# Batch 0's keys by block products, with the sums they need moved ahead of them

## The chip, the core and the metric

The kernel runs on one core of one Trainium2 chip, in 32-bit floats throughout. The metric is the device time of one execution in microseconds (us), given as the median of several runs. In the profile PE is TensorE's matrix multiplier and PEld its weight loads, DVE is VectorE, ACT is ScalarE, POOL is GpSimd, SP is SyncE; a trailing q (SPq, ACTq) is the engine's own instruction queue, where it issues DMAs. L465 is line 465 of the kernel's text.

## The reference

A cross attention with two branches over 16 batches of 100 query rows of width 640, with 8 heads of width 80. Cut to what matters:

```python
enc, ca = encoder_hidden_states[:, :718], encoder_hidden_states[:, 718:]
keyt, valt = enc @ Wk, enc @ Wv                      # (16, 718, 640) each
hs = mha(x @ Wq, keyt, valt)
ca_q1 = einsum('btc,th->bch', ca, Wq_ca)[:, indices]  # 100 of 384 rows
ca_hs1 = mha(ca_q1, x, x)
ca_hs2 = mha(ca_hs1 @ Wq, ca @ Wk_ca, ca @ Wv_ca)
out = (hs + ca_hs2) @ Wout + b_out + x
```

The part that is changed computes keyt for batch 0: the encoder's 718 rows of width 384, times Wk of 384 by 640, kept transposed as the tile kT.

## The kernel before

**Stages.** A prologue (about the first 60 us) loads the weights, makes the values of batch 0 partly (L375), folds the second branch's weights (L1242, L1265), turns Wk (L1288), and makes the keys and queries of batch 0 (L666, L535). Then a loop over the 16 batches: scores (L716), maxima and exponentials, the second branch's softmaxes, and, in between, the keys and values of the following work, so that TensorE has a product to run while the other engines make the softmax. Instructions of the prologue are put into order by a scheduler, which keeps dependences and may move independent instructions; `issue_after(x)` holds a group back until x has been issued on its engine. The loop is issued in the order of the text.

**Keys by 15 block products.** For all batches but the first, the class Keys (L453) makes four of the five 128-row chunks of kT. It takes the encoder rows as three parts u and three width chunks c, and the weights as three chunks c and two halves g, a 3x3 by 3x2 block product. This needs 18 block products written out, and 15 by a scheme of the fast matrix product kind: 15 forms of the inputs (A_AT, enc_sums, L481) times 15 forms of the weights (W_AT, weight_sums, L502), whose products are added up in banks A to E of PSUM and moved to kT by a copy on ScalarE (L407) the first time and by an add on VectorE (L405) after that. K_PLAN lists the order: bank, form, and the part of kT that the bank is added to after it. One block product is two matmul instructions of 240 columns. 13 Pool instructions of 128x240 make a batch's input forms; 12 VectorE instructions of 128x256 make the weights' forms, once. The fifth chunk is made plainly by last_keys (L691): nine instructions with the weights wk4.

**Batch 0's keys before.** first_keys (L684) makes all five chunks plainly through chunk_keys (L661), 5 x 9 matmul instructions of 240 columns, and ten copies on ScalarE (L677). weight_sums was split: the forms that overwrite no raw weights (late=False) run before first_keys' products in the text, the five that do (late=True: 5, 7, 13, 3, 14) after them.

**Second branch of batch 0.** keys(load_m(b)) (L848) writes five masked pieces into the tile m2 on Pool, one for each chunk c. Second.products (L874) multiplies x by them into y_ps, ten instructions; VectorE copies the first T = 4 columns of each head into g (L890), ScalarE the rest into y (L896). scores1 (L898) makes e1 on Pool from g in seven instructions (four products L905, three adds L912), and softmax1 (L916) takes it over on VectorE. m2 is one tile for all batches, so batch 1's masks can only follow batch 0's products.

**Copies of wq.** 15 VectorE copies (L1299, L1305) rearrange wq as its five pieces land, ahead of the weight sums.

**PSUM.** psum() hands out banks of two pools of two in turn (psumk, psum1), which y_ps, w_ps (the turned weights), the kT_ps and k_ps banks, va_ps and q_ps share.

Of the kernel before, what the change touches and what calls it, by code (L numbers as in the profile page):

```python
# [8 lines left out]
F32 = mybir.dt.float32  # L9
AF = mybir.ActivationFunctionType  # L10
ALU = mybir.AluOpType
# [3 lines left out]
B, S, H = 16, 100, 640  # L15
NH, D = 8, 80
CAD, T = 384, 4
SK = 722 - T
P = 128
HC = H // P  # L20
CC = CAD // P
# [32 lines left out]
for h in range(NH):  # L54
    lo = h * D
    while lo < (h + 1) * D:
        c = lo // P
        hi = min((h + 1) * D, (c + 1) * P)
        PIECES.append((h, c, lo - h * D, lo - c * P, hi - lo))
        lo = hi  # L60
# [3 lines left out]
HG = T + HT  # L64
# [58 lines left out]
NF = len(V_PLAN)  # L123
# [3 lines left out]
def kernel(  # L127
# [18 lines left out]
    nc = tc.nc  # L146
# [5 lines left out]
    small = ctx.enter_context(tc.tile_pool(name="small", bufs=1))  # L152
# [18 lines left out]
    def psum1(name):  # L171
        return ps1.tile([P, 512], F32, tag="ps1", name=name)
# [3 lines left out]
    def psum(name):  # L176

        turn[0] += 1
        return (psumk if turn[0] % 2 else psum1)(name)
# [28 lines left out]
    def enc_tile(name):  # L208

        return inp.tile([P, NF, KT], F32, tag="enc", name=name)  # L210

    def rest_tile(name):
        return main.tile([P, len(A_REST), KT], F32, tag="rest", name=name)
# [23 lines left out]
    def a_raw(enc, u, c):  # L237
        if (u, c) in A_REST:
            return enc[1][:, A_REST[u, c]]
        return enc[0][:, A_RAW[u, c]]  # L240

    def a_form(enc, f):
        return enc[0][:, A_AT[f]]
# [8 lines left out]
    wk_sb = const.tile([P, NF, 2, P], F32, name="wk_sb")  # L252
# [11 lines left out]
    enc = enc_tile("enc_0"), rest_tile("rest_0")  # L264
# [216 lines left out]
    def enc_sums(enc):  # L481

        at = lambda f: a_form(enc, f)
        raw = lambda u, c: a_raw(enc, u - 1, c - 1)
        for out, left, right, op in (
            (at(7), raw(2, 3), raw(3, 1), ALU.add),
            (at(11), raw(3, 2), raw(3, 3), ALU.add),
            (at(8), at(11), raw(2, 3), ALU.subtract),
            (at(10), raw(1, 3), at(11), ALU.subtract),
            (at(9), raw(2, 1), raw(2, 2), ALU.add),  # L490
            (at(2), raw(1, 1), at(9), ALU.subtract),
            (at(9), at(9), raw(3, 1), ALU.subtract),
            (at(5), raw(1, 1), raw(2, 1), ALU.subtract),
            (at(5), at(5), raw(2, 3), ALU.add),
            (at(11), raw(1, 3), raw(3, 3), ALU.subtract),
            (at(11), at(11), raw(3, 1), ALU.add),
            (at(4), at(2), at(10), ALU.add),
            (at(4), at(4), raw(1, 2), ALU.add),
        ):
            nc.gpsimd.tensor_tensor(out, left, right, op)  # L500

    def weight_sums(engine, w, late=None, there={}):  # L502


        at = lambda f: there.get(f, w[:, W_AT[f]])
        raw = lambda c, g: w[:, 2 * (c - 1) + g - 1]
        for f, left, right in (
            (0, raw(1, 2), raw(1, 1)),
            (11, raw(2, 2), raw(3, 2)),
            (12, raw(3, 2), raw(3, 1)),  # L510
            (5, raw(2, 2), raw(1, 2)),
            (7, raw(3, 2), at(5)),
            (13, raw(3, 1), at(7)),
            (1, raw(2, 1), raw(3, 1)),
            (3, raw(1, 1), at(7)),
            (6, raw(2, 1), raw(1, 1)),
            (10, raw(3, 1), raw(2, 2)),
            (2, raw(1, 1), raw(2, 2)),
            (14, raw(2, 1), raw(2, 2)),
        ):  # L520
            if late is None or late == (f in (5, 7, 13, 3, 14)):
                engine.tensor_tensor(at(f), left, right, ALU.subtract)


    def queries_tiles(p):
# [135 lines left out]
    def chunk_keys(n, banks, weights, enc):  # L661
        copies = []
        for bank, thirds in zip(banks, ((0, 1), (2,))):
            for i, u in enumerate(thirds):
                for c in range(CC):
                    nc.tensor.matmul(  # L666
                        bank[:, i * KT : (i + 1) * KT],
                        weights[c],
                        a_raw(enc, u, c),
                        start=(i == 0 and c == 0),  # L670
                        stop=(c == CC - 1),
                        skip_group_check=True,
                    )
        for bank, thirds in zip(banks, ((0, 1), (2,))):
            w = len(thirds)
            copies.append(
                nc.scalar.copy(  # L677
                    kT[:, n, thirds[0] : thirds[0] + w],
                    bank[:, : w * KT].rearrange("p (u k) -> p u k", u=w),
                )  # L680
            )
        return copies

    def first_keys(enc):  # L684
        for n in range(HC - 1):
            banks = [psum(f"kT_ps_0_{n}_{k}") for k in range(2)]
            weights = [wk_sb[:, 2 * c + n % 2, n // 2] for c in range(CC)]
            chunk_keys(n, banks, weights, enc)
        last_keys(0, enc)

    def last_keys(b, enc):  # L691
        banks = pair(f"kT_ps_{b}")
        return chunk_keys(
            HC - 1,
            [banks[:, k] for k in range(2)],
            [wk4[:, c] for c in range(CC)],
            enc,
        )
# [140 lines left out]
    def load_m(b):  # L839
        if b < 2:  # L840
            return lambda c: m_sb[c][:, b * HT : (b + 1) * HT]
        mb = small.tile([P, HC, HT], F32, tag="mb", name=f"mb_{b}", bufs=2)
        nc.sync.dma_start(
            out=mb, in_=m_d[:, :, b * HT : (b + 1) * HT].rearrange("c p n -> p c n")
        )
        return lambda c: mb[:, c]

    def keys(m):  # L848

        for c, heads in enumerate(HEADS):  # L850
            n = len(heads)
            nc.gpsimd.tensor_tensor(
                m2[:, c, :n, T:],
                m(c).unsqueeze(1).to_broadcast([P, n, HT]),
                hmask[:, c, :n].unsqueeze(2).to_broadcast([P, n, HT]),
                ALU.mult,
            )

    class Second:

# [13 lines left out]
        def products(self):  # L874

            b = self.b
            y_ps = psum1(f"y_ps_{b}")
            for c, heads in enumerate(HEADS):
                for lo, hi in QC:
                    nc.tensor.matmul(  # L880
                        y_ps[lo:hi, heads[0] * HG : (heads[-1] + 1) * HG],
                        self.xT[:, c, lo:hi],
                        m2[:, c, : len(heads)].rearrange("p h k -> p (h k)"),
                        start=(c == 0),
                        stop=(c == HC - 1),
                        skip_group_check=True,
                    )
            self.g = g = small.tile([S, NH, T], F32, tag="g", name=f"g_{b}")
            y_v = y_ps[:S, : NH * HG].rearrange("p (h k) -> p h k", h=NH)
            summed = nc.vector.tensor_copy(g, y_v[:, :, :T])  # L890
            self.y_v = y_v
            return summed

        def copy(self):
            self.y = y_sbs[self.b % 2]
# [353 lines left out]
    k2T, at = [], 0  # L1249
# [26 lines left out]
        )  # L1276
        nc.sync.dma_start(out=m_d[c], in_=m_sb[c])
    second = Second(0, xT, ca_0)
    keys(load_m(0))
    summed = second.products()  # L1280
    second.copy()
    second.scores1()
    keys(load_m(1))

    for c in range(HC):
        w_ps = psum(f"w_ps_{c}")
        for cc in range(CC):
            nc.tensor.transpose(  # L1288
                w_ps[:, cc * P : (cc + 1) * P], wkt_sb[:, c, cc * P : (cc + 1) * P], ident
            )  # L1290
        act(
            wk_sb[:, c % 2 : 6 : 2, c // 2] if c < HC - 1 else wk4,
            w_ps[:, : CC * P].rearrange("p (a n) -> p a n", a=CC),
        )

    with tc.issue_after(summed.ins):
        for c in range(HC):
            for r in range(2):
                nc.vector.tensor_copy(  # L1299
                    wq_sb[:, c, : 4 * P].rearrange("p (n r k) -> p n r k", n=RG, r=2)[  # L1300
                        :, :, r
                    ],
                    wq_in[c].rearrange("p (r n k) -> p r n k", r=2, n=RG)[:, r, :, :64],
                )
            nc.vector.tensor_copy(  # L1305
                wq_sb[:, c, 4 * P :].rearrange("p (h k) -> p h k", h=NH),
                wq_in[c].rearrange("p (h k) -> p h k", h=NH)[:, :, 64:],
            )
    with tc.issue_after(summed.ins):
        weight_sums(nc.vector, wk_sb, False)  # L1310
    first_keys(enc)
    weight_sums(nc.vector, wk_sb, True)

    va = wide("va")[:, : H // 2]
    va_ps = psum("va_ps")
# [34 lines left out]
    for b in range(B):  # L1350
        p = b // 2
        e_in, now = enc, second
        enc, second = enc_next, second_next
# [220 lines left out]
        for g in range(2):  # L1574
# [3 lines left out]
            order = [(h, i) for h in range(4 * g, 4 * g + 4) for i in range(len(KC))]  # L1578
# [95 lines left out]
```

## Time and profile before

| | |
|---|---|
| three runs | 919.67, 921.84, 922.21 us; median 921.84 |
| the profiled execution | 919.14 us |
| its span, first to last instruction | 917.4 us |
| TensorE's granted clock in it | 0.999 |
| busy in 0 to 30 us | PE 27.14, DVE 10.55, ACT 5.17, POOL 15.22 us |
| busy in 30 to 52 us | PE 22.00, DVE 12.15, ACT 6.84, POOL 17.27 us |

The span is the time from the first to the last instruction on the core; the device time is 1.7 us longer. Rows of a timeline give the start, the duration, the engine, the line, the operation, the tiles written and read, their shape and how many instructions are merged in the row; in brackets stands how long the engine was idle before it and what ended that. Every 32-bit matmul instruction appears as two passes, so that x90 is 45 instructions.

### The profile page before, as it was taken

Reading aid. Unit: us, or ns where it says so; the run is one execution under the profiler, and the core shown is the slowest. Engines: PE = TensorE matmul, PEld = TensorE weight load, DVE = VectorE, ACT = ScalarE, POOL = GpSimd, SP = SyncE. Lnnn points to the kernel's source line nnn. Section 1 sums busy time; section 2 is a strip of 40 time slices with the busy share of each in tenths; the row PEclk is TensorE's granted clock in tenths of the full one; section 3 lists DMA queues with packets and bytes.
Section 4 is the critical chain, followed back from the end, with each engine's and each line's share of the span. In section 5 each row is a group of like instructions: output and inputs, shape, how many; then the busy total and the mean of one; then the engine's idle time right before and its main releaser. Section 6 shows DMA issues by size and latency. Waiting matters only on the chain.

```text
span 917.4 us, 27706 instructions
## 1 busy us (share of the span) xinstructions
PE 910.1 (99%) x11974; PEld 765.7 (83%) x11974; DVE 692.3 (75%) x1116; ACT 434.3 (47%) x836; POOL 706.2 (77%) x659
## 2 busy tenths in 40 slices
PE   9999999999999999999999999999999999999998
PEld 6988889797797979888798787988879788797966
DVE  3459795989759897795967869679785898748883
ACT  2234533737337363652737436264741737426341
POOL 5749999687968879696896969958797687966623
PEclk9999999999999999999999999999999999999999
DMA  9822112031201302230121301203130032210211
GB/s 269 272 77 78 48 32 67 26 104 53 85 28 45 85 29 78 54 100 35 47 60 54 104 32 52 55 24 106 53 81 31 24 106 53 82 46 24 61 45 39
DMA packets 50581, 62.94 MB, mean 69 GB/s; under 512 B 13682, under 2 KB 37810, under 8 KB 50460
## 3 DMA queue, kind: packets, MB, share of 16 engines
q1 hardware_dynamic: 48812, 59.18, 21.6%
q8 instruction: 94, 1.54, 0.7%
q10 hardware_dynamic: 1024, 1.15, 0.4%
q0 software_dynamic: 624, 0.85, 0.3%
q14 instruction: 27, 0.22, 0.1%
HBM read 55.59 MB, written 5.57 MB: 67 GB/s over the span
## 4 chain that ended last, share of the span: by engine, by line
PE 99%; DMA 0%; issue 0%; DVE 0%; POOL 0%; ACTq 0%; POOLq 0%
PE s_ps L716 12%; PE a_ps L1586 12%; PE v_psA L434 11%; PE v_psB L434 9%; PE k_psA L465 8%; PE kT_ps L666 8%; PE k_psB L465 7%; PE o_ps L1164 5%; PE v_psC L434 4%; PE k_psC L465 3%; PE v_ps L375 2%; PE q_ps L593 2%; PE q_ps L535 2%; PE v_psD L434 2%; PE v_psE L434 2%; PE q_psA L593 1%
## 5 line engine op out<-in xcount | busy, mean ns | idle before, releaser
L905 POOL TENSOR_TENSOR e<-ca,g 100x800 f32<-100x800 f32 x64 | 97.9, 1541 | 100.0 <-ACT kT L407 54.6
L500 POOL TENSOR_TENSOR enc<-enc 128x240 f32<-128x240 f32 x135 | 109.0, 817 | 18.3 <-DMA enc<-in_enct 11.1
L1372 DVE TENSOR_TENSOR st<-st,over 120x1600 f32<-120x1600 f32 x48 | 113.3, 2362 | 0.0
L1586 PEld LDWEIGHTS a_ps<-vs,st 120*36 120x36 f32 (+3 forms) x3072 | 109.3, 124 | 3.5 <-issue 3.4
L1586 PE MATMUL a_ps<-vs,st 120*36 120x81 f32 (+3 forms) x3072 | 111.7, 233 | 0.0
L434 PE MATMUL v_psA<-wv_sb,enc 128*120 128x320 f32 x352 | 109.3, 433 | 0.0
L1011 POOL TENSOR_TENSOR hs<-hs,hs 100x640 f32<-100x640 f32 x48 | 94.8, 1974 | 3.8
L912 POOL TENSOR_TENSOR e<-e,e 100x800 f32<-100x800 f32 x48 | 93.6, 1950 | 3.8
L1004 POOL TENSOR_TENSOR hs<-vb,p 100x640 f32<-100x640 f32 x64 | 91.1, 1433 | 3.9 <-DMA vb<-va_d 1.0
L434 PE MATMUL v_psB<-wv_sb,enc 128*120 128x320 f32 x296 | 91.8, 433 | 0.0
L465 PE MATMUL k_psA<-enc,wk_sb 128*128 128x240 f32 x360 | 89.3, 370 | 0.0
L1380 ACT ACTIVATE st<-st 120x1600 f32<-120x1600 f32 x48 | 73.9, 1539 | 29.6 <-DVE st L1372 29.0
L434 PEld LDWEIGHTS v_psA<-wv_sb,enc 128*120 128x120 f32 x352 | 64.2, 183 | 25.0 <-DVE vs L405 0.5
L465 PEld LDWEIGHTS k_psA<-enc,wk_sb 128*128 128x128 f32 x360 | 67.2, 190 | 15.2 <-issue 0.2
L1384 DVE TENSOR_TENSOR most<-most,st 120x800 f32<-120x800 f32 x64 | 65.0, 1015 | 15.4 <-ACT st L766 14.2
L716 PE MATMUL s_ps<-qp,kT 64*56 64x100 f32 (+1 forms) x3072 | 73.1, 248 | 0.0
L465 PE MATMUL k_psB<-enc,wk_sb 128*128 128x240 f32 x300 | 73.0, 366 | 0.0
L434 PEld LDWEIGHTS v_psB<-wv_sb,enc 128*120 128x120 f32 x296 | 54.1, 183 | 21.9 <-DVE vs L405 0.4
L716 PEld LDWEIGHTS s_ps<-qp,kT 64*56 64x56 f32 (+1 forms) x3072 | 66.9, 130 | 5.4 <-issue 4.2
L1079 ACT COPY hsT<-turned_hs 32x160 f32<-32x160 f32 (+7 forms) x244 | 67.7, 278 | 3.0
L772 ACT COPY st<-s_ps 120x800 f32<-120x800 f32 x64 | 49.8, 830 | 34.3 <-PE s_ps L716 34.3
L465 PEld LDWEIGHTS k_psB<-enc,wk_sb 128*128 128x128 f32 x300 | 57.0, 190 | 7.7
(200 smaller groups left out, 1847.0 us busy)
## 6 DMA issues: line engine op xcount, KB each, us to landing
vb<-va_d SPq DMA_DIRECT2D x62, 250.0 KB
enc<-in_enct SPq DMA_DIRECT2D x30, 240.0 KB
enc<-in_enct SPq DMA_DIRECT2D x15, 360.0 KB
xT<-in_xt SPq DMA_DIRECT2D x8, 500.0 KB
rest<-in_enct SPq DMA_DIRECT2D x31, 120.0 KB
xn<-in_x SPq DMA_DIRECT2D x11, 320.0 KB
out<-xn SPq DMA_DIRECT2D x11, 320.0 KB
ca<-in_cas SPq DMA_DIRECT2D x16, 156.2 KB
```

What stands on the lines that cost most here:

```text
L434: nc.tensor.matmul(at[0][j][:KN, : H // 2], a_form(self.enc, f)[:, j * KN : (j + 1) * KN], wv_there.get(f, wv_sb[:, W_AT[f]]), start=first ...
L465: nc.tensor.matmul(at[:, i * KT : (i + 1) * KT], wk_sb[:, W_AT[f], i], a_form(self.enc, f), start=(first and i == 0), stop=last, skip_grou ...
L500: nc.gpsimd.tensor_tensor(out, left, right, op)
L666: nc.tensor.matmul(bank[:, i * KT : (i + 1) * KT], weights[c], a_raw(enc, u, c), start=(i == 0 and c == 0), stop=(c == CC - 1), skip_group ...
L716: nc.tensor.matmul(s_ps[at][k0:k1, cols], w, rhs, start=not begun & {(at, k) for k in range(k0, k1, 32)}, stop=last, skip_group_check=True,)
L905: first = nc.gpsimd.tensor_tensor(to, self.ca[:, t, :].unsqueeze(1).to_broadcast([S, NH, S]), g[:, :, t].unsqueeze(2).to_broadcast([S, NH, ...
L912: nc.gpsimd.tensor_tensor(e, e, to, ALU.add)
L1004: first = nc.gpsimd.tensor_tensor(to, self.vb[t][:S].rearrange("p (h d) -> p h d", h=NH), p2[:, :, t].unsqueeze(2).to_broadcast([S, NH, D] ...
L1011: nc.gpsimd.tensor_tensor(sums, sums, to, ALU.add)
L1372: return nc.vector.tensor_tensor(st[i], st[i], top.over[:KN].unsqueeze(1).to_broadcast([KN, 2, ROWS]), ALU.subtract,)
L1380: nc.scalar.activation(st[i], st[i], AF.Exp, scale=SCALE)
L1586: nc.tensor.matmul(a_v[lo:hi, h % 4], st[i // 2][: KEYS[i], i % 2, h * S + lo : h * S + hi], block(i, h // 4)[: KEYS[i], h % 4], start=(i ...
```

## The change

It makes batch 0's first four chunks of keys by Keys, as for the other batches, and no longer by first_keys. What goes with it:

- enc_sums(enc) for batch 0: 13 more instructions on Pool, in its order ahead of batch 0's masks.
- Batch 0's masks come first, then batch 1's, which are now held until batch 0's last mask has been issued. Before, the scheduler had four of batch 1's ahead of batch 0's last one.
- g is copied in two parts for batch 0: heads 0 to 6 right after the products, head 7 behind all twelve weight sums, and scores1 on Pool reads both.
- All twelve weight sums stand behind the last copy of wq, in one row, ahead of batch 0's products.
- The turned weights are made in the order 4, 0, 1, 2, 3, so that wk4 is there first, and last_keys(0) runs ahead of the block products.
- On SyncE the load of x for batches 2 and 3 (xT) comes ahead of that of batch 1's ca.

From batch 0's scores on, all engines have the same instructions in the same order as before.

```diff
@@ weight_sums
-                engine.tensor_tensor(at(f), left, right, ALU.subtract)
+                made = engine.tensor_tensor(at(f), left, right, ALU.subtract)
+        return made
@@
-    def first_keys(enc):
-        for n in range(HC - 1):
-            banks = [psum(f"kT_ps_0_{n}_{k}") for k in range(2)]
-            weights = [wk_sb[:, 2 * c + n % 2, n // 2] for c in range(CC)]
-            chunk_keys(n, banks, weights, enc)
-        last_keys(0, enc)
-
@@ keys
-            nc.gpsimd.tensor_tensor(
+            made = nc.gpsimd.tensor_tensor(
...
+        return made
@@ Second.products
-            self.g = g = small.tile([S, NH, T], F32, tag="g", name=f"g_{b}")
-            y_v = y_ps[:S, : NH * HG].rearrange("p (h k) -> p h k", h=NH)
-            summed = nc.vector.tensor_copy(g, y_v[:, :, :T])
-            self.y_v = y_v
-            return summed
+            self.g = small.tile([S, NH, T], F32, tag="g", name=f"g_{b}")
+            self.y_v = y_ps[:S, : NH * HG].rearrange("p (h k) -> p h k", h=NH)
+            if b > 0:
+                self.take(0, NH)
+
+        def take(self, lo, hi):
+            return nc.vector.tensor_copy(self.g[:, lo:hi], self.y_v[:, lo:hi, :T])
@@ prologue
-    keys(load_m(0))
-    summed = second.products()
+    enc_sums(enc)
+    masked = keys(load_m(0))
+    second.products()
+    summed = second.take(0, NH - 1)
     second.copy()
-    second.scores1()
-    keys(load_m(1))
-
-    for c in range(HC):
+
+    order = (HC - 1, *range(HC - 1))
+    for c in order:
         w_ps = psum(f"w_ps_{c}")
...
-            nc.vector.tensor_copy(
+            moved = nc.vector.tensor_copy(
                 wq_sb[:, c, 4 * P :].rearrange("p (h k) -> p h k", h=NH),
...
-    with tc.issue_after(summed.ins):
-        weight_sums(nc.vector, wk_sb, False)
-    first_keys(enc)
-    weight_sums(nc.vector, wk_sb, True)
+    with tc.issue_after(moved.ins):
+        made = weight_sums(nc.vector, wk_sb)
+    with tc.issue_after(made.ins):
+        second.take(NH - 1, NH)
+    second.scores1()
+    with tc.issue_after(masked.ins):
+        keys(load_m(1))
+    last_keys(0, enc)
+    Keys(0, enc).go(NF)
```

## The prediction

> **What bounds the kernel now.** First the page: span, engines, the chain that ended last.
>
> ```profile
> span 917.4 us, 27706 instructions
> PE 910.1 (99%) x11974; PEld 765.7 (83%) x11974; DVE 692.3 (75%) x1116; ACT 434.3 (47%) x836; POOL 706.2 (77%) x659
> PE 99%; DMA 0%; issue 0%; DVE 0%; POOL 0%; ACTq 0%; POOLq 0%
> ```
>
> TensorE (PE) is busy 910.1 of 917.4 us and the chain that ended last is 99% PE. A busy PE need not be a PE at its peak, so the second view is who PE waited for, over the whole run.
>
> ```profile
> PE idle_ps L1230 <- DVE idle L1227: 1.1, 1, 1.1
> PE y_ps L880 <- POOL m L852: 0.7, 1, 0.7
> PE z_ps L934 <- issue: 0.6, 2, 0.3
> PE v_ps L375 <- DMA wv_sb<-in_wv: 0.6, 1, 0.6
> PE m_ps L1265 <- issue: 0.5, 1, 0.5
> ```
>
> Its waits come to 3.5 us. Work taken off PE therefore shortens the run one for one, unless a new wait takes its place, and one of these five waits (y_ps on Pool, 0.66 us) lies in the stage that is changed. Third, the chain in order of time through that stage and into batch 0.
>
> ```profile
> 28.61 0.86 POOL m L852 x3
> 29.86 1.46 PE w_ps L1288 x12
> 31.32 18.23 PE kT_ps L666 x90
> 49.55 1.77 PE va_ps L1318 x12
> 82.35 0.81 PE k_psB L465 x4
> ```
>
> Each matmul instruction is recorded as two passes. Batch 0's keys are 45 instructions, 90 passes, 18.23 us: 0.2026 us a pass. The same block products that the change brings to batch 0 already run for batch 1 (k_psB): four passes, 0.81 us, the same price per pass.
>
> **The change part by part.** *Fewer products.* first_keys made 4 chunks of 9 instructions. Keys makes 15 products of 2. That is 6 instructions, 12 passes, 12 x 0.2026 = 2.43 us off PE. The last chunk's 9 instructions stay, and now run first.
>
> *Masks by batch.* Rows of the timeline (start, duration, engine, line):
>
> ```profile
> 27.66 0.69 DVE L1273 COPY m<-m_ps 128x512 f32<-128x512 f32 x1 [0.63 <-PE m_ps L1265]
> 28.31 0.55 PE L1288 MATMUL w_ps<-ident,kT 128*128 128x128 f32 x3
> 28.31 1.16 POOL L852 TENSOR_TENSOR m<-m,hmask 128x96 f32<-128x96 f32 x4
> 29.52 0.34 PE L880 MATMUL y_ps<-m,xT 128*64 128x72 f32 x4 [0.66 <-POOL m L852]
> 30.02 5.28 POOL L852 TENSOR_TENSOR m<-m,hmask 128x64 f32<-128x64 f32 x1 [0.56 <-PE y_ps L880]
> ```
>
> m's last chunk is copied by 28.35, but Pool had batch 1's masks ahead of batch 0's last one, so the last y_ps product waited to 29.52. With batch 0's five first, that mask runs 28.4 to 28.7, before PE has ended its transposes at 28.86: 0.66 us off PE. Everything after it moves up by 0.66: the other 12 transposes end at 31.32 - 0.66 = 30.66, the last chunk's 18 passes (3.65 us) at 34.31.
>
> *Weight sums, now all before the products.* Product one needs form 7, the sixth of the twelve sums. The sums stand on VectorE (DVE) behind the copies of wq.
>
> ```profile
> SPq L1277 <- DMA wq<-in_wq: 0.4, 1, 0.4
> 31.96 0.33 SPq L1277 DMA_DIRECT2D m_d<-m  x1
> 32.17 0.49 DVE L1299 COPY wq_sb<-wq 128x256 f32<-128x256 f32 x2
> 32.71 2.44 DVE L522 TENSOR_TENSOR wk_sb<-wk_sb 128x256 f32<-128x256 f32 x7
> L522 DVE TENSOR_TENSOR wk_sb<-wk_sb x12: 420/425/1912, 32.7 to 48.3; 128x256 f32<-128x256 f32 x12
> ```
>
> The copies too would start 0.66 earlier, but SyncE's store at 31.96 waits 0.4 for the fifth piece of wq to land (the row above it), so its copies start at 31.98 at best, and the sums 0.54 behind (32.71 - 32.17): 32.52. One sum takes 0.425, seven take 2.44, so 0.336 from start to start. The sixth ends at 32.52 + 5 x 0.336 + 0.425 = 34.62; with some 0.1 for the signal PE waits from 34.31 to 34.7. Cost 0.4 us, and between 0 (the piece landed earlier than the store shows) and 1.35 (0.95 of Pool's masks in between, below). I take 0.4, because the store's row is the only one that dates the piece. Forms 13 and 3, the eighth and ninth sums, end at 35.3 and 35.6, and PE needs them at 35.5 and 37.1.
>
> *The products close together.* From 34.7 PE has 30 x 0.405 = 12.15 us of products, to 46.9. Each bank is read by ScalarE or DVE before it is used again:
>
> ```profile
> 83.20 0.56 ACT L407 COPY kT<-k_psB 128x480 f32<-128x480 f32 x1 [0.25 <-PE k_psB L465]
> 84.83 0.66 DVE L405 TENSOR_TENSOR kT<-k_psA,kT 128x480 f32<-128x480 f32 x1
> ```
>
> Nine adds of 0.66 and six copies of 0.56 stand beside 12.15 us of PE. Walking the plan A B D A B E A B A C B C A B C A product by product (E and C are split in two), the tightest is bank B's fourth use: DVE adds A, E, B in a row, 3 x 0.66 us, and ends some 0.3 us before PE comes. I cost it at 0; with each add 0.1 slower PE would lose under 0.1.
>
> *Sums of batch 0's encoder rows: 13 new Pool instructions, ahead of its masks.* Nearest are the same sums for batch 1.
>
> ```profile
> 13.37 0.16 POOL L365 MEMSET y_sb<- 100x8 f32 x2
> 17.24 1.11 SPq L301 DMA_DIRECT2D kT<-in_wkt  x2
> 19.03 0.59 SPq L301 DMA_DIRECT2D kT<-in_wkt  x1
> 23.15 0.29 POOL L852 TENSOR_TENSOR m<-hs_sb,hmask 128x64 f32<-128x64 f32 x1 [9.63 <-DVE hs_sb L1273]
> 58.83 0.69 POOL L500 TENSOR_TENSOR enc<-enc 128x240 f32<-128x240 f32 x1 [11.15 <-DMA enc<-in_enct]
> 106.30 2.80 POOL L500 TENSOR_TENSOR enc<-enc 128x240 f32<-128x240 f32 x2
> ```
>
> Pool is idle from 13.5 to 23.15. Four sums read only what had landed for the values: 13.5 to 16.3 at 0.70. The fifth and sixth need the first third of the rows; the SyncE issues at 17.75, 18.4 and 19.03 each wait for one piece of it, and show no wait, so it is there by then. Nine more at 0.7 end at 23.7 to 25.3. The fourth mask can't start before 27.1 anyway and the third not before 25.8, so there is room of 1 to 2 us, and the cost is 0. DVE's copies there read PSUM; beside DVE work on SBUF a sum takes 1.40 (2.80 for two), and that is a rival.
>
> *g in two parts.* g's last column block comes behind the twelve sums, so Pool's scores1 starts later.
>
> ```profile
> 35.26 3.03 POOL L905 TENSOR_TENSOR e<-ca,g 100x800 f32<-100x800 f32 x2
> 45.69 0.32 SPq L870 DMA_DIRECT2D ca<-in_cas  x1
> 45.74 1.94 POOL L912 TENSOR_TENSOR e<-e,e 100x800 f32<-100x800 f32 x1
> 45.13 3.63 DVE L522 TENSOR_TENSOR wk_sb<-wk_sb 128x256 f32<-128x256 f32 x4 [2.81 <-PE kT_ps L666]
> 48.67 1.01 DVE L807 STREAM_TRANSPOSE turned<-e 128x800 f32<-128x800 f32 x1
> 51.35 1.82 SPq L219 DMA_DIRECT2D enc<-in_enct  x3
> 52.82 0.98 DVE L834 COPY spread<-mx 128x800 f32<-128x800 f32 x1
> 56.34 1.01 DVE L837 STREAM_TRANSPOSE over<-spread 128x800 f32<-128x800 f32 x1 [2.53 <-DMA va_d<-va]
> 63.85 0.88 ACT L927 ACTIVATE e<-e 100x800 f32<-100x800 f32 x1
> ```
>
> The sums end at 32.52 + 11 x 0.336 + 0.425 = 36.6; then g, and what is left of batch 1's masks on Pool (0.6): scores1 runs 37.3 to 49.7 (12.4 us as before), 2.0 later than before. Behind it, one queue at a time. DVE: transpose to spread take 5.1 us (48.67 to 53.8 before), so the next transpose starts at 54.9 and e1 is ready at 56.9; ScalarE reads it at 63.85 - 2.7 = 61.2. SyncE: ca's load waits for scores1's last product, to 47.7, and batch 1's rows behind it for the va products, to 48.7; xT now goes ahead of ca. So the rows still go 2.7 us earlier, and Pool's sums for batch 1 start at 58.83 - 2.7 = 56.1, long after 49.7. Cost 0, with 4 us of cover on the e1 side and 1.0 on ca's; beyond these the delay reaches batch 1's rows first. In exchange no sum sits beside scores1, as the four at 45.13 did, of which one took 1.9 us.
>
> *Sum:* 2.43 + 0.66 - 0.4 = 2.7 us. The profiled execution took 919.14 us (917.4 and 1.7 around the span), so 916.4 by its own measure. It is lower than all three runs (919.67, 921.84, 922.21); the mean of the four executions is 920.7, and from that I forecast **918.0**.
>
> **The rivals.** (1) *The wait for form 7 doesn't come*: wq's fifth piece lands before 31.6. For it: SyncE dates a landing from above only. Gain 3.1: 917.6.
>
> (2) *Pool's masks of batch 1 take turns with DVE.* Three of them (0.29 to 0.35 us) are still queued when DVE begins its copies at 29.4. If each goes between two DVE instructions, form 7 is 0.95 later and the gain is 1.7: 919.0. Against it: the mask at 30.02 needed 5.28 us, because it stood aside until DVE's stream ended at 35.15, and no instruction of that stream got longer. [...]
>
> (3) *Slower: the sums of batch 0 hold Pool past its masks.* If they run at the 1.40 us of the row at 106.30 and the first third lands only at 19.0, nine sums end at 31.6, the five masks (0.32 each) at 33.2, and the last y_ps product goes at 33.25 instead of 29.52: 3.73 lost against 2.43, slower by 1.3: 922.0. It decides once the sums end after 30.3. Against it: DVE works from PSUM there, and the sums beside such work took 0.7.
>
> (4) *The gain is eaten downstream*: e1 or batch 1's rows come late because scores1 starts 2.0 later, and PE waits in batch 0. It needs another 4 us on the e1 side. Time 920.7, no change.
>
> **How the numbers follow.** Forecast 0.66, (1) 0.12, (2) 0.10, (3) 0.07, (4) 0.05. A measurement of this kernel can tell about 0.3% (2.8 us) from no change; the runs shown spread 2.5 us. Against the median 921.84 the bound is 919.1: forecast and (1) end below it about 7 times in 10, (2) about half the time: faster 0.60. (3) and an unknown like it make slower 0.08, and 0.32 stays the same. The range goes from 919.14 - 3.1 = 916.0, less 0.4 of scatter, 915.6, to 922.21 less the 0.9 that the least lucky of the faster cases would leave, 921.3.
>
> **What would show it.** Right: 78 passes between the transposes and va; va's products start near 46.9; y_ps waits for no mask; Pool's batch 0 sums end before 25.8; PE waits 0.3 to 0.5 us for L522 ahead of the first k_psA; scores1 starts near 37; no new PE wait later. Wrong: PE idle ahead of y_ps with Pool still in L500 (3); a wait of over 1 us for L522, with masks between DVE's instructions (2); PE idle ahead of z_ps or batch 1's k_ps (4); kT adds over 0.8 us and PE waiting between the products.

## The result and the profile after

| | before | after |
|---|---|---|
| median of nine runs | 920.94 us (917.72 to 923.77) | 916.66 us (916.04 to 919.66) |
| ratio after to before | | 0.9958, 95% interval 0.9942 to 0.9975 |
| the profiled execution | 919.14 us | 916.04 us |
| its span | 917.4 us | 914.1 us |

Faster by 0.42%, 1.3 us below the forecast of 918.0 and inside its range. Two more sets, run with the experiments on other chips, gave less: 0.9981 (0.9972 to 0.9991) and 0.9980 (0.9970 to 0.9989), 1.7 to 1.8 us by these ratios and 1.4 us between the medians. Both the stage that was meant and a loss behind it can be read in the profile.

First, PE's busy line of the page and PE's waits over the whole run, changed kernel.

```profile
PE 908.2 (99%) x11962; PEld 762.8 (83%) x11962; DVE 699.0 (76%) x1126; ACT 434.2 (47%) x834; POOL 706.8 (77%) x672
```

```profile
PE k_psB L465 <- DVE sm L983: 0.3, 1, 0.3
```

The twelve passes are gone (11974 to 11962), and so is the y_ps wait on Pool. A new one is there that nobody ordered: k_psB, behind a VectorE instruction of batch 0's softmax. Next, rows of the timeline from 13 to 50 us (start, duration, engine, line, operation; in brackets the idle time ahead of it and what ended it).

```profile
17.97 2.00 POOL L500 TENSOR_TENSOR enc<-enc 128x240 f32<-128x240 f32 x3 [1.85 <-DMA enc<-in_enct]
...
23.96 0.29 POOL L846 TENSOR_TENSOR m<-hs_sb,hmask 128x64 f32<-128x64 f32 x1
...
28.48 0.29 POOL L846 TENSOR_TENSOR m<-m,hmask 128x64 f32<-128x64 f32 x1 [0.97 <-PE y_ps L875]
28.84 0.34 PE L875 MATMUL y_ps<-m,xT 128*64 128x72 f32 x4
...
32.44 4.10 DVE L522 TENSOR_TENSOR wk_sb<-wk_sb 128x256 f32<-128x256 f32 x12
33.89 0.57 PE L667 MATMUL kT_ps<-rest,wk 128*128 128x240 f32 x2
34.58 1.08 PE L465 MATMUL k_psA<-enc,wk_sb 128*128 128x240 f32 x4
...
36.69 3.04 POOL L902 TENSOR_TENSOR e<-ca,g 100x800 f32<-100x800 f32 x2 [6.28 <-DVE g L889]
```

Pool's sums end where the first mask starts, at 23.96. The last y product goes at 28.84 (29.52 before). The last chunk's last two passes start at 33.89; two passes take 0.41, so the next could start at 34.3, but k_psA comes at 34.58: 0.3 us of waiting for form 7 (its cause is read off below). From there the products run without a gap, and va follows at 46.93 on the timeline; in the chain of waits it stands at 47.00, before at 49.55: 2.55 us gained.

What made the wait for form 7 can be read from Pool's and VectorE's rows of the same execution, and from SyncE's:

```profile
29.16 1.25 POOL L846 TENSOR_TENSOR m<-m,hmask 128x96 f32<-128x96 f32 x4
...
29.34 0.62 DVE L1297 COPY wq_sb<-wq 128x256 f32<-128x256 f32 x2
...
30.17 0.60 DVE L1297 COPY wq_sb<-wq 128x256 f32<-128x256 f32 x2
...
31.90 0.48 DVE L1297 COPY wq_sb<-wq 128x256 f32<-128x256 f32 x2
...
31.22 0.33 SPq L1274 DMA_DIRECT2D m_d<-m  x1
```

VectorE's fifteen copies of wq run without a gap, so here it waits for no piece of wq; SyncE's store, by which the prediction dated the fifth piece, goes at 31.22, ahead of that piece's copies at 31.90. But the first copies run beside Pool's masks of batch 1: a pair takes 0.62 and 0.60 us, and 0.48 once the masks are over at 30.41. From the first copy to the first sum it is 3.10 us (29.34 to 32.44), against 2.69 in the kernel before (30.02 to 32.71). The masks cost VectorE 0.41 us. Without them the sixth sum would by these rows end at 34.1, before PE is ready at 34.3 (an estimate).

That gain stands until batch 0's loop and shrinks there. The chain in order of time, changed kernel, start and length of each piece:

```profile
63.79 1.51 DVE most L1387
65.32 1.37 DVE most L1387
67.37 0.91 DVE most L1387
68.30 2.22 DVE most L1387
...
80.43 1.05 PE k_psB L465 x4
```

From 60 to 80 us the chain is no longer PE's: it runs through VectorE, above all through its maxima (L1387). In the kernel before, the maxima, Pool's first two products of scores1 and k_psB of the same place stood as follows:

```profile
69.39 2.38 DVE L1384 TENSOR_TENSOR most<-most,st 120x800 f32<-120x800 f32 x2
...
72.03 3.05 POOL L905 TENSOR_TENSOR e<-ca,g 100x800 f32<-100x800 f32 x2
...
82.19 0.97 PE L465 MATMUL k_psB<-enc,wk_sb 128*128 128x240 f32 x4
```

There Pool's products start behind the maxima. Its k_psB started at 82.19, so at 80.43 only 1.76 of the 2.55 us are left.

### The profile page after: what moved, and what is told of

Its sections match the earlier page's. It is cut to its first block, busy times and chain, and to the rows that moved or that the text cites. A ratio compares the mean times of both kernels' runs of the same rounds, so it can differ in the third digit from the quotient of the medians.

```text
span 914.1 us, 27711 instructions
## 1 busy us (share of the span) xinstructions
PE 908.2 (99%) x11962; PEld 762.8 (83%) x11962; DVE 699.0 (76%) x1126; ACT 434.2 (47%) x834; POOL 706.8 (77%) x672
## 3 DMA queue, kind: packets, MB, share of 16 engines
q10 hardware_dynamic: 1024, 1.15, 0.4%
## 4 chain that ended last, share of the span: by engine, by line
PE 96%; DVE 3%; ACT 0%; issue 0%; DVEq 0%
PE a_ps L1589 12%; PE s_ps L710 12%; PE v_psA L434 11%; PE v_psB L434 9%; PE k_psA L465 8%; PE k_psB L465 7%; PE kT_ps L667 6%; PE o_ps L1161 5%; PE v_psC L434 4%; PE k_psC L465 3%; PE q_ps L594 2%; PE q_ps L536 2%; PE v_psE L434 2%; PE v_psD L434 2%; PE v_ps L375 2%; PE q_psA L594 1%
## 5 line engine op out<-in xcount | busy, mean ns | idle before, releaser
L500 POOL TENSOR_TENSOR enc<-enc 128x240 f32<-128x240 f32 x144 | 113.3, 797 | 14.7 <-DMA enc<-in_enct 7.5
L465 PE MATMUL k_psA<-enc,wk_sb 128*128 128x240 f32 x384 | 95.3, 371 | 0.1
L465 PEld LDWEIGHTS k_psA<-enc,wk_sb 128*128 128x128 f32 x384 | 71.5, 190 | 16.3 <-DVE wk_sb L522 0.5
L1387 DVE TENSOR_TENSOR most<-most,st 120x800 f32<-120x800 f32 x64 | 66.3, 1036 | 15.9 <-ACT st L760 14.7
L465 PE MATMUL k_psB<-enc,wk_sb 128*128 128x240 f32 x320 | 78.0, 366 | 0.3 <-DVE sm L983 0.3
L465 PEld LDWEIGHTS k_psB<-enc,wk_sb 128*128 128x128 f32 x320 | 60.7, 190 | 8.6 <-issue 0.7
```

Of the source, the lines that this page charges most:

```text
L465: nc.tensor.matmul(at[:, i * KT : (i + 1) * KT], wk_sb[:, W_AT[f], i], a_form(self.enc, f), start=(first and i == 0), stop=last, skip_grou ...
```

## The experiments

Line numbers of the runs are their own; the operation and the tile say which is which. All runs with a ratio were timed against the kernel before on the same chip.

**hold.** Batch 0 calls scores1 for batch 1 as the later batches do.

```diff
         if b == 0:
-            second.scores1()
+            second.scores1(seen)
```

> The changed kernel, with Pool's first product of batch 1's scores1 held until VectorE's last maximum of batch 0, as the later batches have it. Nothing else moves. Theory: the gain of 2.5 us fell to 1.7 in batch 0's loop because that product, which Pool now starts at 67.5, runs beside the maxima (3.23 us for two, 2.38 before) and VectorE hands the delay on to PE's wait at k_psB. Then the two maxima take 2.4 again, the wait of 0.34 us ahead of k_psB at 80.4 goes, PE starts the scores of batch 1 0.7 to 0.9 us earlier than in the changed kernel, and the span ends near 913.3 by its own profile (ratio to the changed kernel 0.999). Rival: VectorE was late for another reason (the form sums that end earlier, ScalarE); then k_psB still waits and the span stays at 914.1 within 0.3.

Measured: median 916.72 (0.9964, 0.9951 to 0.9976), and on another chip 916.04 (0.9957, 0.9944 to 0.9970; below, hold_2), against 918.19 and 918.71 for the changed kernel on the same chips. Timelines of batch 0's loop follow, for three kernels. Changed kernel, the execution of its first profile:

```profile
67.50 4.41 POOL L902 TENSOR_TENSOR e<-ca,g 100x800 f32<-100x800 f32 x2 [0.56 <-issue]
...
67.28 3.23 DVE L1387 TENSOR_TENSOR most<-most,st 120x800 f32<-120x800 f32 x2
...
80.43 1.05 PE L465 MATMUL k_psB<-enc,wk_sb 128*128 128x240 f32 x4 [0.34 <-DVE sm L983]
```

The run hold:

```profile
70.27 3.04 POOL L902 TENSOR_TENSOR e<-ca,g 100x800 f32<-100x800 f32 x2 [2.58 <-DVE most L1387]
...
68.03 2.01 DVE L1387 TENSOR_TENSOR most<-most,st 120x800 f32<-120x800 f32 x2
...
80.38 0.97 PE L465 MATMUL k_psB<-enc,wk_sb 128*128 128x240 f32 x4
```

With Pool held back 2.58 us, both of its products take 3.04 (not 4.41), the two maxima 2.01 (not 3.23), k_psB doesn't wait, and the gain stays whole: 1.82 us at va (47.66), 1.81 at k_psB. The theory holds for the wait. The span missed it: 914.5, not 913.3, because in this execution va came 0.73 us later than in the first one of the changed kernel, and the pauses told of under before_again were 0.5 us longer. On the size I was low for the median: the profile shows 0.8 us mended, the medians 1.5 and 2.7. The next run says why in part.

**after_again.** The changed kernel, unaltered.

> The changed kernel unaltered. Theory: 2.55 us gained by va's products, 1.7 by the end of batch 0's loop, and the rest up to 3.3 in the first profile came from pauses at the start of k_psA that the kernel before happened to have (1.6 us in six places). If they are scatter of an execution, this profile has pauses of its own in other places, and the ratio stays at 0.994 to 0.998. Rival: they belong to the kernel before and its phase, and this profile has none of them again.

Measured: 918.19 (0.9981, just outside the 0.994 to 0.998 expected). Its timeline:

```profile
68.16 3.04 POOL L902 TENSOR_TENSOR e<-ca,g 100x800 f32<-100x800 f32 x2
...
67.08 4.97 DVE L1387 TENSOR_TENSOR most<-most,st 120x800 f32<-120x800 f32 x2
...
76.38 1.05 PE L465 MATMUL k_psA<-enc,wk_sb 128*128 128x240 f32 x4 [1.15 <-DVE kT L405]
...
81.97 1.05 PE L465 MATMUL k_psB<-enc,wk_sb 128*128 128x240 f32 x4 [0.34 <-DVE sm L983]
```

Here Pool's product started 1.08 us behind the first maximum, when that was just done, and both of Pool's products went ahead of the second: 3.04 us of Pool inside VectorE's 4.97 (2.01 alone). PE waited twice, 1.15 and 0.34 (1.3 and 0.6 by the products' starts, set against those of the kernel before), and of the gain of 2.51 us at va (against before_again) 0.46 was left at k_psB. So the collision costs 0.8 us or 2.05, by the order in which the four instructions go: in the first execution the second maximum went between Pool's two products, here it went behind both. In sum the rows agree with two engines that took turns: 2.01 and 3.04 add up to 5.05, and 4.97 was measured. They don't show why the second maximum, which the trace has begin 0.06 us ahead of Pool's first product (68.10 and 68.16), waited for the second product as well.

**after_2 and hold_2.** The same two kernels once more, side by side on one chip.

> The changed kernel unaltered, once more, on the same chip as the next two. Theory: it loses 0.7 to 2 us of its gain in batch 0's loop in each execution, by as much as Pool's first products happen to meet VectorE's third maximum, and its runs spread by 2 to 3 us: 0.996 to 0.999 of the kernel before.

> The run hold, once more. Theory: 0.7 to 2 us below the changed kernel on the same chip, with no wait in batch 0's loop; ratio to before 0.9955 to 0.997. Rival: the 1.5 us between hold and the changed kernel were scatter of few executions, and the two medians lie within 0.5 us.

Measured: after_2 918.71 (0.9980), its eleven runs from 916.80 to 919.78; hold_2 916.04 (0.9957), the lowest median of the study, its profile without a PE wait behind the prologue. The profiled execution of after_2 was one of its two fastest and shows the light collision (4.41 and 3.23 again). Seven of its eleven runs lie at 918.4 or above, as after_again's profiled one does; I take them for the heavy collision, but only one such execution was profiled. In the first set eight of nine runs lie at 917.4 or below, so that set may hold few heavy ones.

**before_hold.** The edit of hold in the kernel before.

> The kernel before with the one edit of hold: Pool's first product of batch 1's scores1 held until VectorE's last maximum of batch 0. Theory: the collision came with the change, because Pool ends its sums 5 us earlier there; in the kernel before that product starts at 72.0, behind the maximum's end at 71.8 as it is, so the edit does nothing: ratio to before 0.9995 to 1.0005, product at 72.0 to 72.3, no wait ahead of k_psB. Rival: hold gains in any version, 1 us or more here too, and what it mends isn't the change's.

Measured: 919.22 (0.9992, 0.9981 to 1.0002); Pool's product started at 72.46, behind the maxima's end at 72.19 (69.81 and 2.38), and k_psB didn't wait. What hold mends came with the change.

**before_again.** The kernel before, for a second profile.

> The kernel before unaltered, for its profile. If the six pauses ahead of k_psA (1.6 us in all) are scatter, they stand in other batches or are absent; if they belong to that kernel, they are at 161.6, 321.4, 434.8, 761.6, 826.8 and 873.9 again.

Measured: one time, 920.46. The first two profiles differ by 3.3 us in span: 1.7 were left behind batch 0's loop, and 1.6 came later, 1.4 of it in pauses of PE inside z_ps that stand under "issue" (the engine waited for nothing that the profile shows). Rows of the timeline for batch 15, in before_again and in the changed kernel:

```profile
874.62 0.72 PE L934 MATMUL z_ps<-y_sb,e 100*32 100x33 f32 x59
875.91 0.25 PE L934 MATMUL z_ps<-y_sb,e 100*32 100x33 f32 x5 [0.57 <-issue]
```

```profile
870.77 0.75 PE L931 MATMUL z_ps<-y_sb,e 100*32 100x33 f32 x64
871.45 0.65 PE L1088 MATMUL hst_ps<-ident,hs_sb 100*128 100x100 f32 x5
```

From the start of z_ps to that of the next product it is 0.68 us where PE doesn't pause. That time, read for some batches from the timeline of each run, and the sum over all 16:

| run | batch 2 | batch 3 | batch 5 | batch 12 | batch 14 | batch 15 | sum of 16 |
|---|---|---|---|---|---|---|---|
| before | 0.88 | 0.68 | 1.15 | 0.85 | 1.22 | 0.85 | 12.60 |
| before_again | 0.76 | 0.92 | 0.91 | 1.23 | 1.30 | 1.47 | 13.65 |
| before_hold | 1.05 | 0.68 | 0.68 | 0.68 | 1.12 | 1.11 | 12.45 |
| masks_only | 1.07 | 0.68 | 0.77 | 1.24 | 1.06 | 1.18 | 12.79 |
| after | 0.68 | 0.68 | 0.81 | 0.85 | 0.68 | 0.68 | 11.20 |
| after_again | 0.68 | 0.92 | 1.46 | 0.73 | 0.68 | 0.68 | 12.30 |
| hold_2 | 0.68 | 0.92 | 0.71 | 0.69 | 0.68 | 0.68 | 11.33 |
| sums_first | 0.68 | 1.19 | 1.72 | 1.27 | 0.68 | 0.68 | 13.57 |
| g_whole | 0.68 | 0.91 | 0.96 | 0.97 | 0.68 | 0.68 | 11.86 |

Both theories are half right. In batches 3, 5 and 12 the pauses come and go between executions of one kernel. In batches 2, 14 and 15 they are there in each of the four profiles with 18 block products and in none of the ten with 15, which include g_whole, whose loop runs 12 us later than that of the kernel before: it is not the time at which z_ps comes, and the cause must lie in the program as the change leaves it. (The table has nine of the fourteen profiles; in the other five these three batches take 0.68 as well.) Over all batches the four sums have a mean of 12.9 us and the ten one of 12.1: some 0.75 us of the change's gain is made here, by no step that anybody planned. Within each of the two groups the sums scatter by 0.5 to 0.7 us (standard deviation), so the difference of the means is good to some 0.35.

What in the program does it can be read from the traces, though no run was made for it. The pauses stand at fixed places of PE's instruction stream. In batches 3, 5, 10, 12 and 13 a pause, where there is one, comes behind 33, 49, 26, 42 and 23 of z_ps's 64 passes with 18 block products, and behind 46, 62, 39, 55 (54 once) and 36 with 15: 13 passes later each time, about the 12 passes that the change takes off PE ahead of them. In batches 2, 14 and 15 it comes behind 52, 58 and 59 with 18; 13 passes more lie beyond the 64, so with 15 the place has left z_ps. And the pauses go with the loading of instructions. The profile has 94 DMA packets of 16 KB of the kind "instruction" on queue 8. All 41 steps of over 0.2 us between passes inside z_ps end 1.2 to 1.6 us (1.4 in the mean) behind the end of such a packet. So PE most likely waits there for its next instructions, in a stretch where it takes 64 passes and their weight loads in 0.68 us. How late the packet ends differs from execution to execution; where its place lies differs with the program.

**masks_only.** The kernel before with one edit.

```diff
-    keys(load_m(1))
+    with tc.issue_after(masked.ins):
+        keys(load_m(1))
```

> The kernel before, with batch 1's masks held behind batch 0's last one; its 18 block products and the rest stay. Theory: the last y_ps product goes 0.66 us earlier (28.85 for 29.52) and all behind it on PE moves up by as much, so 0.5 to 0.7 us less in the profile at va's products (48.8 for 49.48); against the kernel before a ratio of 0.9993, which the times can hardly tell. Rival: another wait takes its place (wq's pieces or VectorE's copies), and va's products start at 49.4 as before.

Measured: 919.18 (0.9995, 0.9985 to 1.0004). The last y product went at 29.14, in before_again at 29.76, a gain of 0.62 that is still there behind batch 0, and of 0.73 with w_ps in front of it counted, which came 0.11 later. The term is right; the times can't show it.

**no_masks.** hold without that hold of batch 1's masks.

> The run hold, with batch 1's masks not held behind batch 0's last one: Pool takes four of them first, as in the kernel before. Theory: the last y product goes at 29.5 for 28.85 again, but PE's wait for form 7 (0.3 to 0.5 us) shrinks by as much as PE comes later, so only 0.1 to 0.4 of the 0.66 reaches va's products: the two terms of the sum are not independent. Rival: form 7 comes 0.66 later as well (VectorE's stream starts behind the y products) and va's products start 0.66 later.

Measured: 917.37 (0.9974, 0.9964 to 0.9984). PE's rows of the timeline:

```profile
29.52 0.52 PE L1286 MATMUL w_ps<-ident,kT 128*128 128x128 f32 x3 [0.36 <-DMA kT<-in_wkt]
30.48 0.34 PE L875 MATMUL y_ps<-m,xT 128*64 128x72 f32 x4 [0.44 <-POOL m L846]
...
36.54 1.08 PE L465 MATMUL k_psA<-enc,wk_sb 128*128 128x240 f32 x4 [0.44 <-DVE wk_sb L522]
```

In hold these are 29.23 (y_ps) and 35.32 (k_psA). PE came 1.25 us later (0.33 of that stood already at its first y product, 0.43 came with a late piece of wkt, 0.49 with the mask) and waited for form 7 as long as in hold (0.6 us each, from the end of the last chunk's passes to k_psA). By that number my theory failed and the rival came true: VectorE's stream hangs on the y products, through g, and it began 1.25 us later too. But the two waits of 0.6 have different causes, as VectorE's rows show:

```profile
30.98 0.49 DVE L1297 COPY wq_sb<-wq 128x256 f32<-128x256 f32 x2
...
33.84 0.49 DVE L1297 COPY wq_sb<-wq 128x256 f32<-128x256 f32 x2 [0.53 <-DMA wq<-in_wq]
```

Here the masks are over before the copies begin, and from the first copy to the fifth it is 0.73 us, for 1.14 in hold; then VectorE waits 0.53 for wq's fifth piece, for 0.17 in hold. Without that late piece form 7 would by these rows have been ready before PE. So this run doesn't show that the masks' term and the wait for form 7 add up: the same masks, when they are held back, lengthen the copies and make that wait.

**sums_first.** hold with the weight sums ahead of the copies of wq's fifth piece.

```diff
+    with tc.issue_after(summed.ins):
+        for c in range(HC - 1):
+            moved = move(c)
     with tc.issue_after(moved.ins):
         made = weight_sums(nc.vector, wk_sb)
     with tc.issue_after(made.ins):
-        second.take(NH - 1, NH)
+        taken = second.take(NH - 1, NH)
+    with tc.issue_after(taken.ins):
+        move(HC - 1)
```

> The run hold, with VectorE's twelve weight sums and g's last part ahead of the copies of wq's fifth piece, so that they no longer wait for that piece to land. Theory: form 7 was the last to come (PE waited 0.26 us in the changed kernel's profile, 0.5 in hold); now the sums start at 31.9 at the latest, 0.54 earlier, form 7 is ready by 34.0 before PE has ended the last chunk at 34.3, that wait goes, and va's products start 0.3 to 0.6 us earlier than in hold (47.3 there); the copies of the fifth piece, behind g, end near 36.8 and are wanted at 48. Median 0.3 to 0.6 below hold. Rival: PE then waits for the next form or for ScalarE's copies as long, or the kT adds come late, and va starts at 47.3 again.

> The run sums_first, once more. Theory: 0.3 to 0.6 us below hold_2, because PE's wait for form 7 is gone. Rival: that is below what the pauses on PE's side leave to be seen, and the two medians can't be told apart.

Measured: 916.33 (0.9963) and, beside hold_2, 916.60 (0.9958): no gain that can be told. In the first profile k_psA came with no wait to speak of, 0.49 earlier than in hold (where va starts at 47.66, not at the 47.3 of the expectation). In the second the wait was back at 0.64, and VectorE's rows show why:

```profile
32.01 0.50 DVE L1296 COPY wq_sb<-wq 128x256 f32<-128x256 f32 x2 [0.57 <-DMA wq<-in_wq]
...
32.82 0.49 DVE L1296 COPY wq_sb<-wq 128x256 f32<-128x256 f32 x2 [0.18 <-DMA wq<-in_wq]
...
33.37 4.11 DVE L522 TENSOR_TENSOR wk_sb<-wk_sb 128x256 f32<-128x256 f32 x12
```

The third and fourth pieces landed late instead of the fifth. Here the wait for form 7 is wq's landing, which moves from execution to execution. In the first execution of the changed kernel it was Pool's masks.

**g_whole.** hold with g copied at once and scores1 behind the masks.

```diff
-    summed = second.take(0, NH - 1)
+    summed = second.take(0, NH)
     second.copy()
+    second.scores1()
...
-    with tc.issue_after(made.ins):
-        second.take(NH - 1, NH)
-    second.scores1()
```

> The run hold, with g copied whole straight behind the y products and Pool's scores1 behind the masks, so that Pool's products and adds run beside VectorE's twelve weight sums. Theory: a Pool instruction of 1.5 to 1.9 us that has started holds up a sum that VectorE starts behind it (one of the four at 45.13 in the kernel before took 1.9 us for 0.42), so two or three of the first six sums are long, form 7 comes 1.5 to 4 us later, PE waits as much ahead of k_psA, and va starts at 49 to 51. [...]

Measured: 930.17 (1.0105, 1.0089 to 1.0120), 13 us above hold (timed on other chips). Timeline:

```profile
32.40 3.12 POOL L902 TENSOR_TENSOR e<-ca,g 100x800 f32<-100x800 f32 x2
...
32.18 1.94 DVE L1298 COPY wq_sb<-wq 128x256 f32<-128x256 f32 x2
34.05 1.56 DVE L1304 COPY wq_sb<-wq 128x128 f32<-128x128 f32 x1
...
43.18 5.77 DVE L522 TENSOR_TENSOR wk_sb<-wk_sb 128x256 f32<-128x256 f32 x12
...
47.09 1.94 PE L465 MATMUL k_psA<-enc,wk_sb 128*128 128x240 f32 x4 [10.77 <-DVE wk_sb L522]
```

The direction was right and the size far off. I had counted the sums alone; Pool's chain of seven met the copies of wq first. A copy of 0.21 took 1.56 us behind a Pool product, a pair of 0.48 took 1.94, and the stream of copies, 2.7 us long without Pool (five times 0.54), lasted from 31.4 to 43.2; va came at 61.71. PE waited 10.77 us, and its products then ran slow: k_psA's four passes took 1.94 for 1.08. The stretches of 1 to 2 us (sum of busy time for each engine; the granted clock is the third number from the end):

```profile
40.00:41.00 1.00, 0.00 (x0) 0.00 (x0) 1.00 (x1) 0.00 (x0) 1.00 (x1) 0.93 0.05 19
41.00:42.00 1.00, 0.00 (x0) 0.00 (x0) 1.00 (x3) 0.00 (x0) 0.92 (x2) 0.50 0.00 0
...
50.00:51.00 1.00, 1.00 (x4) 0.86 (x3) 0.00 (x0) 0.34 (x1) 0.00 (x0) 0.50 0.09 32
51.00:52.00 1.00, 1.00 (x7) 0.94 (x6) 0.00 (x0) 0.45 (x2) 0.00 (x0) 0.95 0.00 0
```

**sums_twice.** hold with Pool's 13 sums of batch 0 made twice, ahead of the masks; the second time they give the same values.

> The run hold, with Pool's 13 sums of batch 0's rows made twice (the second time they give the same values). By the prediction's third rival, which decides once the sums end after 30.3: they end at 24.0 + 13 x 0.67 = 32.7, the five masks at 34.2, the last y product goes at 34.2 for 28.84, and va starts about 5 us later than in hold, near 52, 2 to 3 us later than in the kernel before (49.5): 921 to 923 us. Rival: part of it lies beside other waits (form 7, wq) and less than 4 us arrive.

Measured: 924.69 (1.0051, 1.0034 to 1.0067). Timeline:

```profile
32.34 1.98 POOL L500 TENSOR_TENSOR enc<-enc 128x240 f32<-128x240 f32 x3
34.28 0.29 POOL L846 TENSOR_TENSOR m<-hs_sb,hmask 128x64 f32<-128x64 f32 x1
...
34.62 1.52 PE L875 MATMUL y_ps<-m,xT 128*64 128x72 f32 x16 [6.38 <-POOL m L846]
36.08 0.90 PE L1287 MATMUL w_ps<-ident,kT 128*128 128x128 f32 x3
```

The sums ended at 34.3, for 24.7 in hold. va came at 55.89, 8.2 us behind hold and 6.4 behind the kernel before; I had said 5, and 2 to 3. The difference of 3.2 is about 1.6 of later end (34.3 for 32.7) and 2.4 of slow clock, less the 0.6 of the wait for form 7 that now lies beside it: y_ps took 1.52 for 0.83, w_ps 0.90 for 0.55, and PE lost 6.63 us against hold where y_ps starts and 9.03 where the last transposes start.

## Why the prediction was right, and where not

**Fewer products, 2.43.** Right. va was forecast near 46.9 and came at 46.93.

**Masks by batch, 0.66.** Right where it was counted: 0.68 in the changed kernel, 0.62 to 0.73 alone (masks_only). But the masks that were held back then ran beside VectorE's copies and made all or part of the next term, so the two terms are not independent.

**The wait for form 7, 0.4 between 0 and 1.35.** Right in place and size: 0.3 to 0.6 us in the profiles of after, after_2, hold, hold_2 and no_masks. In the first profile the size is luck. The prediction took 0.4 because it had wq's fifth piece land at 31.96. The piece was there in time, as the first rival has it, and the masks slowed VectorE, as the second has it, by 0.41 us and not 0.95. The prediction's own cause, a late piece, comes on top in other executions: VectorE waits 0.15 and 0.17 for the fifth in after_2 and hold, 0.53 in no_masks, and 0.57 and 0.18 for the third and fourth in sums_first_2.

**Products close together, 0.** Right: no gap between the products.

**Pool's 13 sums, 0.** Right. They ended at 24.0 to 25.8 in the profiles of after, hold, sums_first and no_masks, at 26.1 in g_whole and 27.0 in sums_first_2, for 23.7 to 25.3 forecast, and no y product waited for them. They ended late where the rows landed late: the fifth sum started at 17.97 to 20.84, when its rows came, and not by 17.75. sums_twice shows that the cover is real and what lies behind it: the third rival's mechanism exists, and its price was too low, because PE, after its wait of 6.38 us there, also ran for a while at half its clock (y_ps took 1.52 us for 0.83).

**g in two parts, 0.** Right for PE in the prologue: scores1 ran from 36.7 to 48.9 (37.3 to 49.7 forecast). What the split avoids was underrated. The second rival, Pool taking turns with VectorE, was set against one row, the mask of 5.28 us that stood aside. g_whole shows the other case: that mask came into a running stream of copies, but where Pool was already at work, a VectorE copy of 0.21 us took 1.56, as long as one of Pool's products there (3.12 for two). In the changed kernel what is left of this is short, the masks of batch 1 (0.3 us each) until 30.41, and its price is the 0.41 us above.

**The step that failed** is the last sentence on g: "Cost 0, with 4 us of cover on the e1 side and 1.0 on ca's". It asked only what would come late. The rows of batch 1 came early: SyncE issued them 2.54 us sooner (2.7 forecast), but Pool's sums began 5.7 us behind the issue and not 7.5, at 54.49 (56.1 forecast, 58.83 before):

```profile
48.81 1.80 SPq L219 DMA_DIRECT2D enc<-in_enct  x3
...
54.49 0.69 POOL L500 TENSOR_TENSOR enc<-enc 128x240 f32<-128x240 f32 x1 [5.64 <-DMA enc<-in_enct]
```

Pool was then through with them before VectorE was through with batch 0's maxima, and its next product, which nothing held back, ran into them. So the fourth rival, a gain eaten downstream, was partly true, by a mechanism that it didn't name; hold shows that it is this one. Why Pool began 1.8 us sooner behind the issue wasn't tested. It isn't the transfer: the rows had been moved by 56.5 in the kernel before and by 54.0 in the changed one, 5.2 us behind the issue in both. In the trace the last of the sixteen signals that tell of the third piece's landing came late, 1.4 us behind the fifteenth, in each of the four profiles with 18 block products (58.32 behind 56.89 in the first), and at most 0.25 behind it in the ten with 15. What delayed it stays open.

**The number.** The sum of 2.7 us was the gain at va within 0.15. The end result is that, less 0.8 to 2.05 us in batch 0, plus some 0.75 in z_ps: 1.2 to 2.5 us, give or take 1 us of pauses. The two later sets show 1.4 by their medians. The first one shows 4.3, more than its own profiles do (3.1 us between the two executions); why it gave more stays open, beyond the few heavy collisions that it may hold. That the forecast of 2.7 lies between them is luck in part: it left out two terms of opposite sign, and one of the terms it had, the wait for form 7, came out by another cause.

## What to carry to other kernels

When an edit makes a stage earlier, look for what now arrives too early as well as for what arrives late: an engine that is off the critical path may start long instructions beside one that is on it. One held instruction (hold) got the loss back, 916.0 to 916.7 us for 918.2 to 918.7. A term that comes out with the right size can still have another cause, so its rows are worth reading again (form 7). A cover should be tested by using it up, and a wait of several us on PE priced with the slow clock that followed it here (about 2 us lost behind the wait of 10.77, 2.4 behind that of 6.38).

## What the runs showed of the hardware

PE's granted clock fell to 0.50 in both runs with a long wait (10.77 us in g_whole, 6.38 in sums_twice). In g_whole the last products ended at 36.3 and the clock fell at about 40.9, 4.6 us later; it was back at about 51, 4 us after the products had begun again at 47.09. In sums_twice the two times are 5.0 us (28.2 to 33.2) and 5.4 (34.62 to 40.0). The two losses were about 2 and 2.4 us. No wait of 1.2 us or less did that: after_again, with its wait of 1.15, and the other eleven profiles have a mean granted clock of 0.999 or 1.000. From one change of the clock to the next it is 30.72 and 10.24 us in g_whole and 6.83 in sums_twice. What sets these times was not shown.

VectorE and Pool drew out each other's instructions, in these three cases those of the one that came second. A mask that came into VectorE's stream of copies took 1.84 us (no_masks) or 2.92 (sums_twice) for 0.29; a copy that came into Pool's stream took 1.56 for 0.21 (g_whole); and four copies that began beside masks already under way took 1.14 us (hold), for 0.73 with no mask running (no_masks).
